# Two-layer graph attention on one core: eight row tiles of the second layer prepared inside the first layer's loop, spread over its odd iterations

## The chip, the cores and the metric

The kernel runs on one core of one Trainium2 chip. The metric is the device time of one execution in microseconds (us), as the median of several runs. The time before the change is 983.33 us (three runs, 982.24 to 983.56). The profiled execution took 982.79 us, and its trace spans 981.0 us.

## The reference

`x` is 4096 x 512 and `adj` is a non-negative 4096 x 4096 matrix, all float32. Two layers follow each other, each with a residual:

```python
# layer 0: attention inside 32 graphs of 128 nodes each
h = relu(layernorm(x))
q, k, v = h @ Wq.T + bq, h @ Wk.T + bk, h @ Wv.T + bv
a = where(mask, q @ k.T * scale, 0)               # mask: both nodes in one graph
scores = (a + adj + adj) * where(mask, 1, -1e6)   # masked softmax over all 4096 columns
x = x + (softmax(scores) * mask) @ v
# layer 1: graph attention with 8 heads of 64
h = relu(layernorm(x))
mx = einsum('nf,hfd->hnd', h, W)                  # per head projection
logits = s_i[:, :, None] + t_j[:, None, :]        # s_i, t_j: mx against two vectors
attn = softmax(where(adj > 0, logits, -inf))
x = x + (attn @ mx, heads side by side)
```

In layer 1 the term `s_i` cancels in the softmax, so a row of the output is a sum over its neighbours j of `exp(t_j) * mx_j`, divided by the sum of `exp(t_j)`. The kernel computes it in this form.

## The kernel before, in words

Rows are handled in 32 tiles of 128. The kernel has four stages.

**Fold.** The query and key weights are multiplied into one matrix (`fold`, L163), so that the scores need one projection and not two.

**Layer 0** is the loop over `g` from 0 to 15 (L523), two row tiles in each iteration. An iteration holds, in program order: the transfer of a later pair of `x` tiles (`load_pair`, L498); the scores of the pair (L464); the projection for the next pair (`queries`, L406, 32 matmuls in the trace); the transpose of the scores and its copy out of PSUM (`turned`, L483 and L485); and for each of the two tiles a pass over a later tile of `adj` (`read`, L425), the product of scores and values with the residual (`attend`, L491 and L493), the store of the new row tile to the DRAM tensor `x1_d` (L496), and the value projection of the next pair (`values`, L418, 8 matmuls for each tile). At its end the pair after the next is normed and transposed (`normed`, L121 and L127).

`read` takes a tile of `adj` in two halves of 1 MB from a ring of seven buffers (`AB = 7`). VectorE turns each half into bytes (L136), ScalarE reads it with an exponential whose sum is the masked part of the denominator (L441, the tile `junk`), and the bytes go to the DRAM tensor `a_d` (L447).

**Preparing layer 1.** For each row tile `normed1(i)` loads the row tile from `x1_d` (L362), norms it (VectorE L114 and L116, GpSimd L118 and L120, VectorE L121), transposes it on TensorE (L127) and takes it out of PSUM on ScalarE (L128). `prepare(i, ...)` projects it (L244, 16 matmuls in the trace, into two PSUM tiles `pp`), takes the exponential of `t_j` (ScalarE L372), multiplies the projection with it (VectorE L253, twice), and splits the result into two float32r parts (ScalarE L231, GpSimd L232), which stay in SBUF as `part0` to `part31`. A tile is always normed one step ahead of its projection. `row1`, `hT1` and `e` have two buffers each (pool `sb2`). The projections share four PSUM buffers (`pp`, pool `ps_p`) with `queries`, `values` and `attend`.

Before the change the only iteration of the loop that does such work is the last one: `prepare_on` (L536) acts if `last`. Its four calls norm tiles 0 to 3 and prepare tiles 0 to 2. The other 29 are prepared in a loop of their own after layer 0 (L567). Parts 0 to 7 lie in the pool `lo`, in memory that the fold has left. Parts 8 to 31 lie in the pool `hi`, which is opened when layer 0's pools are closed (L562) and uses their memory. The weights of the projection, `w1x`, are loaded and extended on VectorE by `load_w1` (L149, products L157 and sums L158), in iteration 2.

**Aggregating layer 1** (L588): for each of 32 row tiles the bytes of `adj` come back from `a_d` (`mw`, L266), VectorE transposes them in blocks (L271) and casts them (L278), and TensorE multiplies them with all parts (L284, 96 matmuls for each tile). A check that the graphs are the row tiles (`graphs_are_tiles`, L300 on) belongs to the second tile of this loop.

The order on each engine is not the order of the source alone. A scheduler orders the instructions when the kernel is built: it takes the earlier line first among those that its model of the engines holds ready. It fixes one order for each engine[...]. So the first block transposes of the aggregation and the check of the graphs stand among the instructions of the preparation.

Of the kernel before, what the change touches and what calls it, by code (L numbers as in the profile page):

```python
# [51 lines left out]
def kernel(  # L52
# [96 lines left out]
    def load_w1(pool, tmp):  # L149

        w = pool.tile([P, KC, WX], F32, name="w1x")
        nc.sync.dma_start(w[:, :, :D], w1.rearrange("(k p) m -> p k m", p=P))
        a_sb = tmp.tile([P, D], F32, name="a_sb", bufs=1)
        nc.sync.dma_start(a_sb, a_dst.to_broadcast([P, D]))
        for k in range(KC):
            wa = tmp.tile([P, D], F32, name="wa", bufs=1)
            nc.vector.tensor_tensor(wa, w[:, k, :D], a_sb, ALU.mult)  # L157
            nc.vector.tensor_reduce(  # L158
                w[:, k, D:], wa.rearrange("p (h d) -> p h d", d=HD), AX.X, ALU.add
            )  # L160
        return w
# [180 lines left out]
    with ExitStack() as straight:  # L342
# [4 lines left out]
        with ExitStack() as prep:  # L347
# [3 lines left out]
            def part_tile(pool, j):  # L351
                if j >= LO:
                    return pool.tile([P, CB, 2, CW1], F32R, name=f"part{j}")
                if j % 2 == 0:
                    two.append(pool.tile([P, 2, CB, 2, CW1], F32R, name=f"part{j}", tag="lo"))
                return two[-1][:, j % 2]
# [3 lines left out]
            def normed1(i):  # L360
                row = sb2.tile([P, D], F32, name="row1")
                nc.sync.dma_start(row, x1_d[i])  # L362
                norm(row, row)
                hT = sb2.tile([P, KC, P], F32, name="hT1")
                relu_T(ps_t, row, hT)
                return hT

            def prepare(i, hT, part):
                pm = project1(ps_p, hT, w1x)
                e = sb2.tile([P, EW], F32, name="e")  # L370
                nc.gpsimd.memset(e[:, EC:], 1.0)
                nc.scalar.activation(e[:, ES:EC], pm[1][:, HW : HW + H], AF.Exp)  # L372
                nc.gpsimd.tensor_copy(e_all[:, i, :], e[:, ES:EC])
                weigh(e, pm)
                split(e, part)
                parts.append(part)

            with (
# [21 lines left out]
                def queries(hT):  # L400

                    gT = sb.tile([P, KC, G * P], F32, name="gT")
                    for m in range(KC):
                        pp = ps_p.tile([P, D], F32, name="pp")
                        for k in range(KC):
                            nc.tensor.matmul(  # L406
                                pp[:, : G * P], m_sb[:, k, ts(m, P)], hT[:, k, :],
                                start=(k == 0), stop=(k == KC - 1),
                            )
                        nc.scalar.activation(  # L410
                            gT[:, m, :], pp[:, : G * P], AF.Identity, bias=c_sb[:, m : m + 1]
                        )
                    return gT
# [11 lines left out]
                def read(i, diag, sums):  # L425


                    a8 = sb.tile([P, N], FP8, name="a8", bufs=3)
                    n = 1
                    for h in range(2):  # L430
                        a, base = aa[2 * i + h], h * NH
                        mask_bytes(a8, a, h)
                        own = i * P - base
                        pieces = ((0, NH),)
                        if 0 <= own < NH:
                            nc.gpsimd.tensor_copy(diag, a[:, ds(own, P)])
                            pieces = ((0, own), (own + P, NH))
                        for c0, c1 in pieces:
                            if c0 < c1:
                                junk = sb.tile([P, NH], BF16, name="junk", bufs=1)  # L440
                                nc.scalar.activation(  # L441
                                    junk[:, c0:c1], a[:, c0:c1], AF.Exp, scale=2.0 * NEG,
                                    accum_out=sums[:, n : n + 1],
                                )
                                n += 1
                        if h:
                            nc.sync.dma_start(a_d[i], a8.bitcast(F32))  # L447
                        if 2 * i + h + AB < 2 * NT:
                            aa[2 * i + h + AB] = load_adj(ap, 2 * i + h + AB)
                    return n  # L450

                def seen():
                    return (
                        sb.tile([P, G, P], F32, name="diag", bufs=3),
                        [small.tile([P, 4], F32, name="sums", bufs=8) for _ in range(G)],
                        [],
                    )

                def scores(g, hT, gT, r, diag, sums, counts):

                    pss = ps_s.tile([P, G, P], F32, name="pss")
                    for t in range(G):
                        for k in range(KC):
                            nc.tensor.matmul(  # L464
                                pss[:, t, :], gT[:, k, ts(t, P)], hT[:, k, ts(t, P)],
                                start=(k == 0), stop=(k == KC - 1),
                            )
                    s = sb.tile([P, G, P], F32, name="s")
                    nc.vector.scalar_tensor_tensor(s, diag, 2.0, pss, ALU.mult, ALU.add)
                    for t in range(G):  # L470
                        nc.scalar.activation(
                            s[:, t, :], s[:, t, :], AF.Exp, bias=r[:, t : t + 1],
                            accum_out=sums[t][:, 0:1],
                        )
                        rsum = rs_all[:, G * g + t : G * g + t + 1]
                        nc.vector.tensor_reduce(rsum, sums[t][:, : counts[t]], AX.X, ALU.add)
                        nc.vector.reciprocal(rsum, rsum)
                    return s

                def turned(s):  # L480
                    ps = ps_s.tile([P, G, P], F32, name="pss")
                    for t in range(G):
                        nc.tensor.transpose(ps[:, t, :], s[:, t, :], ident)  # L483
                    sT = sb.tile([P, G, P], F32, name="sT")
                    nc.scalar.copy(sT, ps)  # L485
                    return sT
# [11 lines left out]
                def load_pair(g):  # L498
                    xg[g] = sb.tile([P, G, D], F32, name="xg", bufs=3)
                    nc.sync.dma_start(  # L500
                        xg[g], x[g * G * P : (g + 1) * G * P, :].rearrange("(t p) d -> p t d", p=P)
                    )
# [20 lines left out]
                for g in range(NG):  # L523
                    last = g + 1 == NG
                    if g + 2 < NG:
                        load_pair(g + 2)
                    if g == 2:
                        w1x = load_w1(pool1, sb)
                    nlook = seen()

                    def look_on(t):
                        if not last:
                            i = G * (g + 1) + t
                            nlook[2].append(read(i, nlook[0][:, t, :], nlook[1][t]))

                    def prepare_on():  # L536
                        if last:
                            i = len(ahead)
                            ahead.append(normed1(i))
                            if i:  # L540
                                prepare(i - 1, ahead[i - 1], part_tile(lo, i - 1))

                    s = scores(g, hT, gT, r, *look)
                    prepare_on()
                    prepare_on()
                    if not last:
                        ngT = queries(nhT)
                    sT = turned(s)
                    nvs = []
                    for t in range(G):  # L550
                        look_on(t)
                        attend(sT, vs[t], g, t)
                        prepare_on()
                        if not last:
                            nvs.append(values(nhT, t))
                    if not last:
                        hT, r, gT, vs, look = nhT, nr, ngT, nvs, nlook
                    if g + 2 < NG:
                        nhT, nr = normed(g + 2)
# [347 lines left out]
```

## Time and profile before

| stage (chain of waits) | from, us | to, us |
|---|---|---|
| start, fold, first norms | 0 | 56.16 |
| layer 0, iterations 0 to 14 | 56.16 | 340.15 |
| iteration 15 and preparation | 340.15 | 480.30 |
| aggregation, end | 480.30 | 981.0 |

| engine | busy us | share of the span |
|---|---|---|
| TensorE matmul | 947.1 | 97% |
| VectorE | 461.6 | 47% |
| ScalarE | 261.6 | 27% |
| GpSimd | 180.3 | 18% |

The profile page gives the busy time of each engine, and cuts the span into 40 slices with the busy share, the granted TensorE clock and the traffic of the DMA engines. The chain of waits is the chain of work that ended last, followed back from the end. The timeline lists the instructions of one engine in order, with the idle time ahead of each and the instruction that ended it. A loop iteration can be found in these views by its scores matmuls (L464), which stand at 56.16, 74.86, 93.56, 113.43 and so on up to 340.15 us.

### The profile page before, as it was taken

Reading aid. Unit: us, or ns where it says so; the run is one execution under the profiler, and the core shown is the slowest. Engines: PE = TensorE matmul, PEld = TensorE weight load, DVE = VectorE, ACT = ScalarE, POOL = GpSimd, SP = SyncE. Lnnn points to the kernel's source line nnn. Section 1 sums busy time; section 2 is a strip of 40 time slices with the busy share of each in tenths; the row PEclk is TensorE's granted clock in tenths of the full one; section 3 lists DMA queues with packets and bytes.
Section 4 is the critical chain, followed back from the end, with each engine's and each line's share of the span. In section 5 each row is a group of like instructions: output and inputs, shape, how many; then the busy total and the mean of one; then the engine's idle time right before and its main releaser. Section 6 shows DMA issues by size and latency. Waiting matters only on the chain.

```text
span 981.0 us, 13168 instructions
## 1 busy us (share of the span) xinstructions
PE 947.1 (97%) x5051; PEld 820.8 (84%) x5051; DVE 461.6 (47%) x982; ACT 261.6 (27%) x501; POOL 180.3 (18%) x344
## 2 busy tenths in 40 slices
PE   6899999999999998999999999999999999999995
PEld 4477666766776676888899999999999999999995
DVE  3756866776675287655232423324233242342421
ACT  3676666676671222333100000000000000000000
POOL 1111211221121055555201101011010110101100
PEclk9899999999999998999999999999999999999998
DMA  9949898998992142222013133131221312312111
GB/s 347 419 181 370 352 370 333 377 367 346 368 371 77 59 129 80 65 65 70 6 43 87 50 81 83 47 86 50 80 85 45 86 51 80 86 44 86 50 38 36
DMA packets 58043, 148.28 MB, mean 151 GB/s; under 512 B 6387, under 2 KB 23027, under 8 KB 49779
## 3 DMA queue, kind: packets, MB, share of 16 engines
q1 hardware_dynamic: 48178, 130.31, 38.2%
q10 hardware_dynamic: 9792, 17.05, 4.6%
q8 instruction: 41, 0.67, 0.3%
q14 instruction: 32, 0.25, 0.1%
HBM read 113.77 MB, written 33.55 MB: 150 GB/s over the span
## 4 chain that ended last, share of the span: by engine, by line
PE 86%; DMA 4%; DVE 4%; ACT 3%; POOL 1%; issue 1%; SPq 0%; ACTq 0%; DVEq 0%
PE pg L284 50%; PE pp L418 10%; PE pp L244 9%; PE pp L406 8%; PE pp L491 3%; DMA a<-adj 3%; PE pss L464 2%; PE pt L127 2%; PE pp L190 2%; ACT junk L441 1%; DMA xg<-x 1%; ACT gT L410 1%; POOL part L232 1%; DVE row L121 1%; POOL rstd L120 0%
## 5 line engine op out<-in xcount | busy, mean ns | idle before, releaser
L284 PE MATMUL pg<-part,at 128*128 128x348 f32 x3072 | 489.0, 321 | 1.2 <-DVE e L253 1.2
L284 PEld LDWEIGHTS pg<-part,at 128*128 128x128 f32 x3072 | 488.7, 188 | 1.6 <-issue 1.6
L278 DVE CAST at<-at 128x4096 fp32r<-128x4096 fp8e4 x32 | 73.6, 2301 | 311.6 <-PE pg L284 311.6
L291 ACT COPY tot<-pg 128x522 f32<-128x522 f32 x32 | 19.1, 598 | 469.9 <-PE pg L284 469.9
L441 ACT ACTIVATE junk<-a 128x2048 bf16<-128x2048 f32 (+15 forms) x92 | 124.6, 1355 | 37.4 <-DMA a<-adj 19.4
L244 PE MATMUL pp<-w1x,hT 128*128 128x256 f32 (+1 forms) x512 | 119.5, 387 | 0.0
L418 PE MATMUL pp<-wv,hT 128*128 128x512 f32 x256 | 116.8, 599 | 1.0 <-ACT hT L128 1.0
L406 PE MATMUL pp<-hT,m_sb 128*128 128x256 f32 x512 | 113.2, 379 | 0.0
L244 PEld LDWEIGHTS pp<-w1x,hT 128*128 128x128 f32 x512 | 96.5, 193 | 14.3 <-issue 0.5
L406 PEld LDWEIGHTS pp<-hT,m_sb 128*128 128x128 f32 x512 | 96.1, 190 | 12.9 <-issue 0.5
L418 PEld LDWEIGHTS pp<-wv,hT 128*128 128x128 f32 x256 | 49.1, 193 | 62.0 <-issue 60.4
L136 DVE TENSOR_SCALAR a<-a 128x512 fp8e4<-128x512 f32 x256 | 94.6, 453 | 7.3 <-DMA a<-adj 4.7
L593 POOL COPY den_all<-tot 128x1 f32<-128x1 f32 x31 | 5.8, 186 | 368.2 <-DVE tot L292 368.2
L128 ACT ACTIVATE hT<-pt 128x512 f32<-128x512 f32 x64 | 37.7, 599 | 82.3 <-PE pt L127 82.3
L602 POOL TENSOR_TENSOR tot<-tot,row 128x512 f32<-128x512 f32 x31 | 40.0, 1289 | 62.0 <-DVE tot L297 62.0
L118 POOL TENSOR_SCALAR ve<-mv 128x1 f32<-128x1 f32 x64 | 16.2, 255 | 178.6 <-DVE mv L116 164.8
L232 POOL TENSOR_TENSOR part<-e,part 128x522 fp32r<-128x522 f32 x32 | 42.0, 1312 | 31.4 <-ACT part L231 27.8
L422 DVE TENSOR_TENSOR v<-pp,bv_sb 128x512 f32<-128x512 f32 x32 | 22.1, 691 | 42.3 <-PE pp L418 42.3
L271 DVE STREAM_TRANSPOSE at<-mw 128x1024 f32<-128x1024 f32 x32 | 39.6, 1238 | 0.0
L253 DVE TENSOR_TENSOR e<-pp,e 128x256 f32<-128x256 f32 x64 | 26.7, 418 | 25.3 <-ACT e L372 22.8
L410 ACT ACTIVATE gT<-pp,c_sb 128x256 f32<-128x256 f32 x64 | 29.9, 469 | 31.5 <-PE pp L406 31.4
L120 POOL TENSOR_TENSOR rstd<-ve,neghalf 128x1 f32<-128x1 f32 x64 | 36.8, 578 | 4.6
(94 smaller groups left out, 594.7 us busy)
## 6 DMA issues: line engine op xcount, KB each, us to landing
a<-adj SPq DMA_DIRECT2D x64, 1024.0 KB, 11.9
a_d<-a SPq DMA_DIRECT2D x32, 512.0 KB, 10.2
row<-x_d SPq DMA_DIRECT2D x64, 256.0 KB, 3.4
mw<-a_d SPq DMA_DIRECT2D x128, 128.0 KB, 4.0
xg<-x SPq DMA_DIRECT2D x16, 512.0 KB, 4.6
x_d<-x ACTq DMA_DIRECT2D x32, 256.0 KB, 4.3
out<-tot ACTq DMA_DIRECT2D x31, 256.0 KB, 3.8
wkT_sb<-wkT SPq DMA_DIRECT2D x4, 256.0 KB, 4.6
```

Source lines behind the costliest of these rows:

```text
L128: nc.scalar.activation(dst, pt, AF.Relu)
L136: nc.vector.tensor_scalar(a8v[:, u], av[:, u], 0.0, None, ALU.is_gt, saturate=False)
L232: nc.gpsimd.tensor_sub(dst[:, :, 1, :], e3, dst[:, :, 0, :].bitcast(F32))
L244: nc.tensor.matmul(pm[g][:, :n], hT[:, k, :], w1x[:, k, g * HW : g * HW + n], start=(k == 0), stop=(k == KC - 1),)
L271: nc.vector.transpose(at8.rearrange("p c n b -> p (c n b)").bitcast(F32).rearrange("p (c u n) -> p c u n", c=NW, n=B), mw.rearrange("p u ( ...
L278: nc.vector.tensor_copy(at.rearrange("p (c b) q -> p c b q", b=BY), at8.rearrange("p c q b -> p c b q"))
L284: nc.tensor.matmul(pg[:, c, : 2 * CW1], at[:, j, :], part(j)[:, c].rearrange("p s w -> p (s w)"), start=(j == 0), stop=(j == NT - 1),)
L406: nc.tensor.matmul(pp[:, : G * P], m_sb[:, k, ts(m, P)], hT[:, k, :], start=(k == 0), stop=(k == KC - 1),)
L410: nc.scalar.activation(gT[:, m, :], pp[:, : G * P], AF.Identity, bias=c_sb[:, m : m + 1])
L418: nc.tensor.matmul(pp, hT[:, k, ts(t, P)], wv[:, k, :], start=(k == 0), stop=(k == KC - 1))
L441: nc.scalar.activation(junk[:, c0:c1], a[:, c0:c1], AF.Exp, scale=2.0 * NEG, accum_out=sums[:, n : n + 1],)
L602: nc.gpsimd.tensor_add(num, num, row)
```

## The change

`prepare_on` takes a condition. It is called in three places: after the scores in the last iteration; after `turned` in the odd iterations from 3 to 15; and after the first `attend` in the last iteration. So iterations 3, 5, 7, 9, 11 and 13 each norm one row tile of layer 1 and prepare the one before it (iteration 3 only norms tile 0), which prepares tiles 0 to 4. The last iteration prepares tiles 5, 6 and 7 and norms up to tile 8. The loop after layer 0 begins at tile 8 and has 24 tiles, where it had 29. The weights `w1x` are loaded in iteration 1. The purpose is to give TensorE work of layer 1 during layer 0, from row tiles that are long finished, and to leave less of it for the stage between the layers.

```diff
@@ -524,7 +524,7 @@
-                    if g == 2:
+                    if g == 1:
                         w1x = load_w1(pool1, sb)
@@ -533,24 +533,24 @@
-                    def prepare_on():
-                        if last:
+                    def prepare_on(now):
+                        if now:
                             i = len(ahead)
                             ahead.append(normed1(i))
                             if i:
                                 prepare(i - 1, ahead[i - 1], part_tile(lo, i - 1))
 
                     s = scores(g, hT, gT, r, *look)
-                    prepare_on()
-                    prepare_on()
+                    prepare_on(last)
                     if not last:
                         ngT = queries(nhT)
                     sT = turned(s)
+                    prepare_on(3 <= g and g % 2)
                     nvs = []
                     for t in range(G):
                         look_on(t)
                         attend(sT, vs[t], g, t)
-                        prepare_on()
+                        prepare_on(last and t == 0)
                         if not last:
                             nvs.append(values(nhT, t))
```

## The prediction

> **What bounds the kernel now.** I read the page first, for which engine is full and where.
>
> ```profile
> PE 947.1 (97%) x5051; PEld 820.8 (84%) x5051; DVE 461.6 (47%) x982; ACT 261.6 (27%) x501; POOL 180.3 (18%) x344
> PE   6899999999999998999999999999999999999995
> PEclk9899999999999998999999999999999999999998
> ```
>
> TensorE is busy 97% of the span. Its only slice after the start that falls short is the sixteenth (about 368 to 392 us), and the clock row dips there too. That is the passage from layer 0 to the preparation. A change that adds no TensorE work and removes none can gain only what TensorE loses: it stands idle or runs at a lower clock. So the question is how much it loses in each stage that the change touches. The timeline of TensorE shows an idle gap only where it has one. Layer 0 has four of note:
>
> ```profile
> 104.19 0.66 PE L127 MATMUL pt<-ident,hn 128*128 128x128 f32 x4 [1.28 <-DVE hn L121]
> 160.90 1.12 PE L491 MATMUL pp<-v,sT 128*128 128x512 f32 x2 [0.27 <-ACT sT L485]
> 199.55 1.12 PE L491 MATMUL pp<-v,sT 128*128 128x512 f32 x2 [1.32 <-ACT sT L485]
> 238.09 1.12 PE L491 MATMUL pp<-v,sT 128*128 128x512 f32 x2 [1.19 <-ACT sT L485]
> ```
>
> The first is iteration 2, where the extension of `w1x` takes VectorE ahead of a norm. The other three lie in iterations 5, 7 and 9, each at the first `attend`, which waits for the copy of the turned scores. The timeline of ScalarE tells why that copy is late at 199:
>
> ```profile
> 196.65 0.63 ACT L441 ACTIVATE junk<-a 128x512 bf16<-128x512 f32 x1 [0.72 <-DMA a<-adj]
> 197.41 1.38 ACT L441 ACTIVATE junk<-a 128x1408 bf16<-128x1408 f32 x1
> 199.14 0.36 ACT L485 COPY sT<-pss 128x256 f32<-128x256 f32 x1
> ```
>
> ScalarE's fixed order puts a read of `adj` ahead of the copy, and the read waits for its transfer. As a check, the scores of iteration 0 stand at 56.16 us and those of iteration 15 at 340.15 us. That is 283.99 us for 15 iterations. An undisturbed one takes 132.13 - 113.43 = 18.70 us, so 15 take 280.5, and layer 0 loses 3.5 us in all. The gaps of iterations 5, 7 and 9 are 0.27 + 1.32 + 1.19 = 2.8 us of it.
>
> The passage between the stages loses more (timeline of TensorE, then stretches of 4 us with clock):
>
> ```profile
> 357.57 0.66 PE L127 MATMUL pt<-ident,row 128*128 128x128 f32 x4 [1.24 <-DVE row L121]
> 371.39 1.12 PE L127 MATMUL pt<-ident,row 128*128 128x128 f32 x4 [3.27 <-DVE row L121]
> 389.46 0.66 PE L127 MATMUL pt<-ident,row 128*128 128x128 f32 x4 [0.49 <-DVE row L121]
> ```
>
> ```profile
> 368.00:372.00 4.00, 0.73 (x4) 0.61 (x4) 3.58 (x9) 0.71 (x2) 2.70 (x8) 0.82 0.11 20
> 372.00:376.00 4.00, 4.00 (x14) 3.33 (x13) 3.04 (x9) 1.49 (x3) 0.73 (x2) 0.50 0.21 68
> 376.00:380.00 4.00, 4.00 (x16) 3.34 (x16) 2.69 (x5) 0.40 (x2) 1.52 (x3) 0.83 0.51 147
> ```
>
> In a row the columns are TensorE, weight loads, VectorE, ScalarE, GpSimd, then the clock. After a gap of 3.27 us the clock is 0.50 for 4 us and 0.83 for 4 more, which costs 2.0 + 0.7 = 2.7 us beyond the gap. From 340.15 to 393.0 us (52.9 us) TensorE projects ten tiles. In the even stretch after it a tile takes 3.95 us (the chain has its projections at 401.07, 405.01, 408.96). Ten tiles and the scores, transposes and products of iteration 15 (1.79 + 0.2 + 1.9) come to 43.4 us. So the passage loses about 9.5 us. Of that 5.2 are idle gaps on `row L121` and about 3 are clock. From 393 to 479 us nothing is lost.
>
> [...] 0.50 after a gap of 3.27 us, and 1.00 around the gaps of 1.2 to 1.3 us in layer 0. [...] the split L232 (median 1.23 us) took 3.22 us at 352.88, under the cast L278. [...]
>
> **The change, part by part.**
>
> Moved: five tiles of preparation (29 after the loop become 24). On TensorE that is 5 x 3.95 = 19.7 us taken from after layer 0 and added inside it. The sum on TensorE is zero. The last iteration prepares three tiles before and after.
>
> Gaps of iterations 5, 7 and 9: the call is placed behind `turned` and ahead of the first `attend`, in odd iterations. So 3.5 us of projections (16 matmuls) come to stand between the turned scores and the `attend` that waits for their copy. The copy may then be 3.5 us later without a gap, and the three gaps are at most 1.32 us. Also, every odd iteration grows by 3.95 us while the bytes of `adj` stay the same, so the reads wait less. I count -2.8 us; the bounds are -2.8 and 0.
>
> Other engines in layer 0: one tile costs VectorE 0.69 + 0.18 + 0.55 + 2 x 0.42 = 2.3 us (L114, L116, L121, L253), up to 3.2 where L121 takes 1.44 as it does at 369.90; ScalarE 0.60 + 0.18 + 0.63 = 1.4 us; GpSimd 0.22 + 0.57 + 1.23 + 0.3 = 2.3 us. VectorE is busy 14.3 of 20 us there, or 13.4 of an iteration of 18.7; an odd iteration has 13.4 + 3.2 = 16.6 of 22.65. ScalarE has 12.7 + 1.4 = 14.1. Neither becomes the bound, and the cost is hidden under TensorE.
>
> Added waits. The transposes of a row tile of layer 1 wait for L121. Its row was stored two or more iterations earlier and its transfer takes 3.4 us, so it can be ready long before. The two `pp` buffers of a projection come free only after L372 and both L253, which stand behind reads of `adj` in the lists of ScalarE and VectorE. Behind them TensorE has the first `attend` and the first `values` on the other two buffers, 0.86 + 3.43 = 4.3 us, and then the second `attend` wants one of the two. A read that waits longer than that would stop TensorE. The waits of `junk` on `a<-adj` total 14.7 us in 21 waits, the longest 1.8 us. So mostly nothing, sometimes one gap like those of now. The bounds are 0 and five gaps of 1.3 us = 6.5 us; I take +0.8.
>
> `w1x` one iteration earlier: the same 4 products and 4 sums of 0.68 us, against the same kind of norm. I take 0, with the present gap of 1.28 us as bound to either side.
>
> The passage: what disturbs it stays. The block transposes (three of 1.23 us), casts (two of 2.3 to 2.5 us) and the check of the graphs (16 operations of 0.42 us) are 15 us of VectorE work, which stands in its list among the norms. Their first input waits for memory of layer 0 to come free, so they come when layer 0 ends, now or after the change. A norm must be ready every 3.95 us, and a row must be loaded (3.4 us), normed (about 3) and transposed within two tiles, 7.9 us. That leaves about 1 us for foreign work. So again several us are lost. The order will be a new one, and the long gap with its half clock (6 us together) may be shorter or double. In favour of shorter: in the last iteration there is one row fewer to norm. I take -0.7, with bounds of -6 and +6.
>
> Tiles 8 on now come straight after layer 0, into memory that layer 0 has just left. The last store of `x1` takes 4.3 us to land, while the first split into that memory comes about 8 us after the last `attend` (projections of tiles 7 and 8). I take 0, and up to 3 us if it is held.
>
> Sum: -2.8 + 0.8 + 0 - 0.7 + 0 = -2.7, so 983.3 - 2.7 = 980.6 us.
>
> **The rivals.**
>
> A, the forecast above (gaps of layer 0 go, the passage stays about as it is): about 980.6, chance 0.40.
>
> B, the passage gets through without a gap long enough to lower the clock. It then loses about 3.5 where it lost 9.5, and layer 0 gains 2: 983.3 - 6 - 2 = 975.3. For it: one gap makes up most of the loss. Against it: the same VectorE work comes at the same place. Chance 0.20.
>
> C, new gaps in layer 0 on `pp` or on the copies cost what the old ones did, and nothing else moves: 983. For it: VectorE and ScalarE run close behind their transfers. Against: their slack above. Chance 0.15.
>
> D, slower: the new order in the passage has a second long gap, or the first splits wait for layer 0's memory: +6 and -2 give 987. For it: a pair of tiles has only about 1 us of slack, and the loop after layer 0 loses its five tiles in memory that is free from the start. Against: nothing is added there. Chance 0.25.
>
> **How the numbers follow.** Faster by over 0.2% means below 981.4. All of B, most of A (0.34) and little of C give 0.56. Slower by over 0.2% is above 985.3: D, with some of it inside the bound, and a little of C, 0.25. The rest is 0.19. The range takes in B and D: 974 to 987.5.
>
> **What would show it.** Right: no gap on the copy `sT` (L485) in iterations 5, 7 and 9; the scores of successive iterations 18.70 and 22.65 us apart in turn from iteration 4 on; gaps on `row L121` of some 5 us in the passage with the clock at 0.5 once. Wrong: gaps in odd iterations ahead of the second `attend` or at `queries`; ScalarE's L231 waiting for a store at tile 8; a passage with no half clock, or with two.

## The result and the profile after

| | before, us | after, us | ratio, 95% interval |
|---|---|---|---|
| measured with the prediction (4 runs each) | 983.44 | 980.59 | 0.9967, 0.9944 to 0.9989 |
| measured again (41 and 13 runs) | 983.12 | 980.2 | 0.997, 0.9956 to 0.9985 |

The change makes the kernel about 3 us faster, 0.3%. The profiled execution after the change spans 976.9 us, 4.1 us less than the one before.

Three rows of the page of the changed kernel:

```profile
PE 944.0 (97%) x5051; PEld 818.9 (84%) x5051; DVE 460.5 (47%) x982; ACT 260.1 (27%) x501; POOL 185.2 (19%) x344
PE   6899999999999998899999999999999999999995
PEclk9799999999999999999999999999999999999998
```

TensorE runs the same 5051 matmuls. Its busy row still falls below nine tenths in the slices of the passage, now the sixteenth and seventeenth. The clock row no longer dips there. The timeline of TensorE after the change shows these gaps from the first scores to the last projection (the number in brackets is the idle time ahead of the instruction, then what ended it):

```profile
86.78 1.12 PE L491 MATMUL pp<-v,sT 128*128 128x512 f32 x2 [1.24 <-ACT sT L485]
143.82 1.12 PE L491 MATMUL pp<-v,sT 128*128 128x512 f32 x2 [0.56 <-ACT sT L485]
227.30 1.12 PE L491 MATMUL pp<-v,sT 128*128 128x512 f32 x2 [0.80 <-ACT sT L485]
373.82 0.65 PE L127 MATMUL pt<-ident,row 128*128 128x128 f32 x4 [0.38 <-DVE row L121]
387.42 0.66 PE L127 MATMUL pt<-ident,row 128*128 128x128 f32 x4 [3.02 <-DVE row L121]
396.30 0.66 PE L127 MATMUL pt<-ident,row 128*128 128x128 f32 x4 [1.20 <-DVE row L121]
404.17 0.66 PE L127 MATMUL pt<-ident,row 128*128 128x128 f32 x4 [1.53 <-DVE row L121]
```

The gaps of iterations 5, 7 and 9 are gone. The first three rows are iterations 1, 4 and 8, all without projections. The gaps of layer 0 come to 2.6 us, where they were 4.1 us. In the passage the gaps remain: 6.1 us in sum, where they were 5.2 us. So the passage did not gain from shorter gaps.

Where the time went, by the starts of the scores of iterations 0 and 15 and the start of the aggregation:

| | before, us | after, us | difference |
|---|---|---|---|
| start to scores of iteration 0 | 56.0 | 56.9 | +0.9 |
| iterations 0 to 14 | 284.0 | 301.4 | +17.4 |
| iteration 15 and preparation | 140.3 | 117.9 | -22.4 |
| aggregation, end | 500.7 | 500.7 | 0.0 |

The work that moved is five projections of 3.51 us and the transposes of six row tiles of 0.44 us, 20.2 us in all. (The transposes of one row tile and a quarter stood ahead of iteration 15 before the change, and those of seven and a quarter do now.) Layer 0 grew by 17.4 us for it, so layer 0 runs 2.8 us better. The passage shrank by 22.4 us, so it runs 2.2 us better in this pair of profiles; the experiments show that this second part is the clock of the two executions. The start is not touched by the change; it lay between 53.7 and 57.7 us in the profiles of this study.

The gain in layer 0 of 2.8 us is more than the 1.5 us by which its gaps fell. The chain of waits of the changed kernel shows iteration 6, without projections, and iteration 7, with them:

```profile
183.71 0.47 ACT gT L410
184.19 0.27 ACT sT L485
184.46 0.04 issue
184.50 1.12 PE pp L491 x2
...
203.03 3.51 PE pp L244 x16
206.54 0.87 PE pp L491 x2
```

In iteration 6 the chain leaves TensorE for the copies on ScalarE, and the first `attend` takes 1.12 us; the iteration lasts 18.70 us. In iteration 7 the projections run up to the `attend`, which takes 0.87 us. Iteration 7 lasts 22.31 us, although 18.70 + 3.95 would be 22.65. From these numbers an undisturbed iteration holds a wait of about 0.34 us that its timeline doesn't list as a gap, and the projections cover that too. The experiment `odd_scores` below tests this.

### The profile page after: what moved, and what is told of

Read it like the earlier page. It is cut to its first block, busy times and chain, and to the rows that moved or that the text cites. A ratio compares the mean times of both kernels' runs of the same rounds, so it can differ in the third digit from the quotient of the medians.

```text
span 976.9 us, 13164 instructions
## 1 busy us (share of the span) xinstructions
PE 944.0 (97%) x5051; PEld 818.9 (84%) x5051; DVE 460.5 (47%) x982; ACT 260.1 (27%) x501; POOL 185.2 (19%) x344
## 4 chain that ended last, share of the span: by engine, by line
PE 87%; DMA 4%; DVE 3%; ACT 2%; POOL 2%; issue 1%; SPq 0%; ACTq 0%; DVEq 0%; POOLq 0%
PE pg L284 50%; PE pp L418 10%; PE pp L406 9%; PE pp L244 8%; DMA a<-adj 3%; PE pp L491 3%; PE pss L464 2%; PE pt L127 2%; PE pp L190 2%; ACT junk L441 1%; POOL part L232 1%; DMA xg<-x 1%; DVE row L121 0%; DVE a L136 0%; ACT gT L410 0%
## 5 line engine op out<-in xcount | busy, mean ns | idle before, releaser
L244 PE MATMUL pp<-w1x,hT 128*128 128x256 f32 (+1 forms) x512 | 117.3, 383 | 0.0
L128 ACT ACTIVATE hT<-pt 128x512 f32<-128x512 f32 x64 | 37.0, 598 | 76.6 <-PE pt L127 76.4
```

The lines of the kernel that those rows point to most:

```text
L128: nc.scalar.activation(dst, pt, AF.Relu)
L244: nc.tensor.matmul(pm[g][:, :n], hT[:, k, :], w1x[:, k, g * HW : g * HW + n], start=(k == 0), stop=(k == KC - 1),)
```

## The experiments

Layer 0 and the passage of each profiled execution are set side by side first. To compare them, the moved work is taken out of layer 0 and added to the passage (20.2 us where eight tiles are prepared before the loop behind layer 0, 19.6 us for `even`, which has transposed fewer row tiles by then, 12.3 us for `half`). Beside each stands what TensorE lost there: the sum of its listed gaps, and the time that the half clock cost (half of its length: 1.7 us where the clock was 0.50 for 3.4 us).

| kernel | time, us | layer 0 less moved work | gaps, clock | passage plus moved work | gaps, clock |
|---|---|---|---|---|---|
| before | 983.12 | 284.0 | 4.1, 0 | 140.3 | 5.2, 3.4 |
| `w1_only` | 986.07 | 286.7 | 5.3, 1.7 | 139.2 | 5.2, 1.7 |
| changed | 980.59 | 281.2 | 2.6, 0 | 138.1 | 6.1, 0 |
| `after_again` | 980.2 | 281.3 | 2.8, 0 | 139.2 | 5.6, 1.7 |
| `w1_late` | 979.56 | 280.7 | 2.5, 0 | 139.2 | 5.5, 1.7 |
| `half` | 980.88 | 282.8 | 3.9, 0 | 139.1 | 5.5, 1.7 |
| `odd_scores` | 982.05 | 282.9 | 2.9, 0 | 138.9 | 5.6, 1.7 |
| `even` | 981.65 | 286.4 | 6.6, 1.7 | 139.1 | 5.6, 1.7 |
| `before_graphs` | 978.96 | 284.5 | 4.9, 0 | 134.9 | 3.0, 0 |
| `after_graphs` | 975.71 | 280.7 | 2.2, 0 | 133.8 | 2.3, 0 |
| `graphs_w2` | 975.63 | 280.5 | 2.3, 0 | 133.7 | 2.3, 0 |
| `after_graphs_row3` | 978.3 | 286.2 | 6.3, 1.7 | 131.8 | 0.8, 0 |
| `graphs_row3_w2` | 978.38 | 286.2 | 4.6, 3.4 | 131.8 | 0.8, 0 |
| `graphs_row3_w3` | 976.73 | 282.1 | 3.7, 0 | 131.8 | 0.8, 0 |

The experiments ran on three chips. The kernel before took 983.12, 982.65 and 983.43 us on them, and each ratio below is against the kernel before on the same chip.

The table is nearly a sum. Take 279.9 us (layer 0 of the kernel before without its gaps), add the gaps and the lost clock, and take off 0.34 us for each iteration that has projections behind `turned`: this meets layer 0 of all fourteen profiles within 0.4 us. The passage without its gaps and lost clock is 131.0 to 132.3 us in all of them.

**The changed kernel once more: is the passage better, or only its clock?** No edit.

> The changed kernel itself, profiled and timed once more. If the gain is a saving in layer 0 (theory 1: the projections fill TensorE's wait between the turned scores and the first attend in odd iterations), the stretch from the scores of iteration 0 to those of iteration 15 is again about 301.4 us, and the time is 980 to 981. If the gain hangs on the clock not falling in the passage (theory 2), this profile may show a half clock after a gap of some 3 us there, the passage is then some 3 us longer, and the time of some executions is near 983.

Measured: 980.2 us, ratio 0.997 (0.9956 to 0.9985). Layer 0 took 301.5 us. The passage took 1.1 us longer than in the first profile. Stretches of 4 us, where the third number from the end is the clock; first the changed kernel, then its second profile:

```profile
384.00:388.00 4.00, 0.98 (x7) 0.59 (x6) 3.07 (x7) 0.70 (x2) 3.67 (x10) 1.00 0.01 1
388.00:392.00 4.00, 4.00 (x22) 3.42 (x21) 3.46 (x9) 2.00 (x4) 1.04 (x2) 1.00 0.51 131
```

```profile
384.00:388.00 4.00, 1.32 (x6) 0.78 (x5) 3.07 (x6) 0.70 (x2) 3.86 (x7) 1.00 0.18 43
388.00:392.00 4.00, 3.66 (x15) 3.15 (x16) 3.46 (x11) 0.60 (x1) 1.25 (x5) 0.66 0.20 66
```

The same gap of 3.02 us is followed by a clock of 1.00 once and by 0.66 the other time, with 22 and 15 matmuls in the next stretch. Theory 1 holds for layer 0. Of theory 2 remains that the difference between the two executions' passages is the clock, 1.7 us, less 0.6 us of shorter gaps: they have the same list of instructions.

**The earlier load of `w1x` alone.**

```diff
-                    if g == 2:
+                    if g == 1:
                         w1x = load_w1(pool1, sb)
```

> The kernel before with w1x loaded in iteration 1, and nothing else. Theories 1 and 2: the gap of 1.28 us moves from iteration 2 to 1, the gaps of iterations 5, 7 and 9 stay, and the time is 983.4 within 1 us. Theory 3 (the earlier load is what helps): 981 or less.

Measured: 986.07 us, ratio 1.003 (1.0017 to 1.0043). This misses all theories: it is slower by some 3 us. Layer 0 of the profile is 2.7 us longer: its gaps grew by 1.2 us, and behind the gap of 2.09 us the clock was at half for 3.4 us, which cost 1.7. The timeline of TensorE shows these gaps, and one more of 0.48 us in iteration 6:

```profile
87.17 1.12 PE L491 MATMUL pp<-v,sT 128*128 128x512 f32 x2 [1.08 <-ACT sT L485]
200.41 1.13 PE L491 MATMUL pp<-v,sT 128*128 128x512 f32 x2 [1.02 <-ACT sT L485]
221.47 1.12 PE L491 MATMUL pp<-v,sT 128*128 128x512 f32 x2 [2.09 <-ACT sT L485]
298.06 1.13 PE L491 MATMUL pp<-v,sT 128*128 128x512 f32 x2 [0.58 <-ACT sT L485]
```

The gap at 221 is in iteration 8, long after the load. The copy `sT` needs these transposes of TensorE, which end at 218.5 us:

```profile
218.12 0.38 PE L483 MATMUL pss<-ident,s 128*128 128x128 f32 x2
```

The timeline of ScalarE there, first of this kernel and then of the kernel before in the same iteration:

```profile
218.79 1.91 ACT L441 ACTIVATE junk<-a 128x2048 bf16<-128x2048 f32 x1 [1.20 <-DMA a<-adj]
...
221.06 0.36 ACT L485 COPY sT<-pss 128x256 f32<-128x256 f32 x1
```

```profile
217.51 0.36 ACT L485 COPY sT<-pss 128x256 f32<-128x256 f32 x1
...
218.28 1.90 ACT L441 ACTIVATE junk<-a 128x2048 bf16<-128x2048 f32 x1
```

Before, the copy comes ahead of a read of `adj`; here a read that waits for its transfer comes ahead of the copy, which starts some 2.6 us after its input is there. So an edit in iteration 1 gives ScalarE another order seven iterations later, and TensorE waits for it. Its passage has the same gaps as before (1.24, 3.27, 0.19 and 0.48 us).

**The same tiles, the call in another place.**

```diff
-                    prepare_on(last)
+                    prepare_on(last or (3 <= g and g % 2))
...
-                    prepare_on(3 <= g and g % 2)
+                    prepare_on(last)
```

> The changed kernel with the same tiles in the same odd iterations, but the call placed after the scores and ahead of the queries. Theory 1: the first attend has its wait for the copy of the turned scores back, so an odd iteration is 18.70 + 3.95 = 22.65 us and not 22.31, and gaps ahead of the first attend of odd iterations can come back; layer 0 is 2 to 4 us longer than in the changed kernel, 303.4 to 305 us, and the time about 983. Theory 2 (the place does not matter, only the passage does): layer 0 stays at 301.4 and the time follows the passage.

Measured: 982.05 us, ratio 0.9995 (0.9982 to 1.0008). Layer 0 took 303.05 us, a little under the range of theory 1. Iterations 5, 7, 11 and 13 took 22.64, 22.53, 22.99 and 22.64 us, where the changed kernel has 22.31 or 22.32 in each of them. The chain of waits of this kernel in iteration 7:

```profile
206.81 0.22 PE pss L483 x2
207.03 0.66 PE pt L127 x6
207.69 1.08 PE pp L491 x2
```

The `attend` has its longer duration back, 1.08 us. Of the gain of 2.9 us only about 1 is left, and the interval includes none. In the profile it is 1.1 us, just what the listed gaps fell by (4.1 to 2.9 us); there is no gap in iterations 5, 7 and 9 here either. The place behind `turned` carries the rest, the five waits of 0.34 us, as theory 1 has it.

**Even iterations.**

```diff
-                    prepare_on(3 <= g and g % 2)
+                    prepare_on(last or (4 <= g and g % 2 == 0))
```

> The changed kernel with the calls after turned in iterations 4, 6, 8, 10, 12 and 14 and not in the odd ones. The same tiles are moved. Theory 1: an even iteration becomes 22.31 us as the odd one was, so layer 0 again saves about 0.36 us for each of five tiles; the gaps on the copy now fall where no projections stand, up to 1.3 us each: layer 0 is 301 to 304 us. If the odd iterations were needed (the reads of adj late in just those), it is at the upper end. The passage has another order; its loss is open between 4 and 10 us, and so is the time, 979 to 986.

Measured: 981.65 us, ratio 0.9992 (0.9977 to 1.0006). Layer 0 of the profiled execution took 306.1 us, beyond the range expected. But that execution took 984.37 us, 2.7 us above the median, and 1.7 us of its layer 0 are a half clock of 3.4 us behind the first gap below. Iterations 6 and 10 took 22.32 us, so the small saving is there. The gaps of layer 0 by the timeline of TensorE:

```profile
87.68 2.07 PE L491 MATMUL pp<-v,sT 128*128 128x512 f32 x2 [2.58 <-ACT sT L485]
146.40 1.12 PE L491 MATMUL pp<-v,sT 128*128 128x512 f32 x2 [0.62 <-ACT sT L485]
207.80 0.44 PE L127 MATMUL pt<-ident,row 128*128 128x128 f32 x2 [1.75 <-DVE row L121]
291.60 1.12 PE L491 MATMUL pp<-v,sT 128*128 128x512 f32 x2 [1.65 <-ACT sT L485]
```

The second is in iteration 4, which only norms a tile, and the last in iteration 11; no projections stand in either. The third, in iteration 7, is a wait of the added work itself, for the norm of a row of layer 1. By the medians the odd places are the better ones, by about 1.5 us; the single times of `even` lie between 979.2 and 987.8 us, so the size is not well known. Why iteration 1 lost 2.58 us here and 1.24 in the changed kernel was not separated.

**The spread alone.**

```diff
-                    if g == 1:
+                    if g == 2:
                         w1x = load_w1(pool1, sb)
```

> The changed kernel with w1x loaded in iteration 2 as before, so with the spread preparation alone. If the earlier load costs in the changed kernel what it cost alone (layer 0 2.7 us longer), layer 0 is some 299 us and the time 977.5. If the longer odd iterations take that cost up, layer 0 stays at 301.5 and the time at 980.2. If tile 0 now waits for w1x in iteration 5, layer 0 is longer by 1 us or more.

Measured: 979.56 us, ratio 0.9961 (0.9947 to 0.9975). Layer 0 took 300.9 us, 0.5 us less than in the changed kernel. So the earlier load, which cost 3 us by itself, costs about half a microsecond beside the spread in these profiles; the intervals of the times overlap and don't show it. It is the spread preparation that gains, 3.1 us alone. Layer 0 gained 3.3 us by the table, and its two parts make up the whole: the gaps fell from 4.1 to 2.5 us, and five waits of 0.34 us are 1.7 us.

**Half of it.**

```diff
-                    prepare_on(3 <= g and g % 2)
+                    prepare_on(7 <= g and g % 2)
```

> The changed kernel with calls in iterations 7, 9, 11 and 13 only, so three tiles prepared in layer 0 and six before the loop behind it, where the changed kernel has five and eight. Theory 1 (a saving of 0.34 us for each odd iteration with projections, and the gaps on the copy in them): relative to the changed kernel two savings of 0.34 are lost and the gaps of iterations 5 and 7, up to 1.5 us together, can come back; iterations 9, 11 and 13 are 22.31 us and iteration 5 is 18.70 or more. The time is 981 to 982.5. If the saving lies in the passage alone, the time is again 980.2.

Measured: 980.88 us, ratio 0.9978 (0.9965 to 0.9991), just under the range expected. Iterations 9, 11 and 13 took some 22.32 us each; iterations 6, 7 and 10, without projections, had gaps of 0.76, 0.84 and 0.97 us. The passage has the same four gaps (0.38, 3.02, 0.62 and 1.53 us) as with eight tiles. How many tiles are moved does not change what the passage loses.

**What the passage loses: the check of the graphs moved into layer 0.** The check is the same, in 16 pairs of half the size, and `held` is set at the start.

```diff
+                    if g == 13:
+                        graphs_are_tiles(sb)
...
             if i == 1:
-                graphs_are_tiles(sb3)
```

> The changed kernel with the check of the graphs done in iteration 13 of layer 0 (in 16 pairs of half the size, which a full SBUF asks for) and not in the passage. If the gaps on row L121 come from foreign VectorE work among the norms, 6.6 us less of it leave gaps of 2 to 4 us where there are 5.6 to 6.1, and no half clock if the gap of 3.0 us is one of those that shrink: passage 114.5 to 117 us where it is 118 to 119, time 977 to 978.5. [...]

Measured: 975.71 us, ratio 0.9932 (0.9918 to 0.9945), better than expected. The passage took 113.6 us, some 5 us less. In this run's timeline of TensorE (its lines stand one further down: L128 is L127):

```profile
371.59 0.66 PE L128 MATMUL pt<-ident,row 128*128 128x128 f32 x4 [0.38 <-DVE row L122]
383.84 0.66 PE L128 MATMUL pt<-ident,row 128*128 128x128 f32 x4 [1.91 <-DVE row L122]
```

Two gaps of 2.3 us in sum are left of four with 5.6 to 6.1, and the clock stays at 1.00. VectorE work of 6.6 us among the norms cost 3.3 to 3.8 us of gaps and the clock behind them. Part of this gain is lost again: the aggregation takes 502.1 to 503.0 us in the six kernels with the moved check, and 500.6 to 501.1 us in the others. Why was not separated.

**The same in the kernel before.** The same edit on the kernel before.

> The kernel before with the check of the graphs done in iteration 13 and not in the passage; nothing is spread. If the passage's gaps have the same cause in both kernels (the check among the norms), the passage shrinks as it did in the changed kernel, by about 5 us to 134 to 136, layer 0 stays at 284, and the time is 977.5 to 979: then the spread preparation and this are independent, and each adds its own gain. If the spread preparation was what made room for the check, this gains 2 us or less.

Measured: 978.96 us, ratio 0.9963 (0.9949 to 0.9976). The passage took 134.9 us, 5.4 us less, and layer 0 284.5 us. The gaps of the passage fell from 5.2 to 3.0 us, and the clock stayed at 1.00. Moving the check and spreading the preparation add up: on the same chip the spread kernel with the moved check (`graphs_w2`, below) took 975.63 us, which is again about 3 us for the spread.

**A third row buffer.** `bufs=3` for `row1`, on top of the moved check. To make room, `w1x` is extended in halves of 256 columns.

```diff
-                row = sb2.tile([P, D], F32, name="row1")
+                row = sb2.tile([P, D], F32, name="row1", bufs=3)
```

> The same with three buffers for row1 and not two (and w1x extended in halves of 256 columns, to make room). If the gaps come from the round of a row (load 3.4 us, norm about 3, transpose) in two tiles, a third buffer gives about 4 us more slack, and the gaps of the passage nearly go: passage 112.5 to 114.5 us, time 974.5 to 977. If VectorE is simply full at these moments, or the norm's order is fixed too late, it changes nothing against the run with the check moved alone.

Measured: 978.3 us, ratio 0.9951 (0.9935 to 0.9968), slower than expected. The passage shrank to 111.6 us, even a little more than expected; one gap is left in it:

```profile
388.00 0.66 PE L128 MATMUL pt<-ident,row 128*128 128x128 f32 x4 [0.78 <-DVE row L122]
```

But layer 0 took 306.4 us, with gaps of 2.33 and 1.76 us in iterations 1 and 2 and a half clock of 3.4 us behind the first. The next three runs move the load of `w1x` (`g == 2` or `g == 3` in the place of `g == 1`), first without and then with the third buffer.

> The changed kernel with the check moved and w1x loaded in iteration 2. If the parts add up: 975.7 less the 0.6 us that the later load gave, so 974.5 to 976.

Measured: 975.63 us, ratio 0.9933 (0.9913 to 0.9953), as expected, and not to be told from `after_graphs`. These two are the fastest here.

> The same with the third row buffer and w1x extended in halves. In the run with w1x in iteration 1 the passage was 111.6 us but layer 0 had two gaps of 2.3 and 1.8 us and a half clock at the extension. If the later place avoids these, layer 0 is 301 us and the time 972 to 974.5. If extending in halves costs them wherever it stands, layer 0 is 304 to 306 and the time about 978.

Measured: 978.38 us, ratio 0.9951 (0.9936 to 0.9967). Layer 0 again took 306.4 us: four gaps of 3.3 us in sum and a half clock of 6.8 us now lie in iterations 2 and 3.

> The same with w1x in iteration 3, which is still two iterations ahead of its first use. As the run before, 972 to 974.5 if the place decides; if tile 0's projection in iteration 5 waits for the extension, there is a gap at L244's first matmuls there.

Measured: 976.73 us, ratio 0.9942 (0.9922 to 0.9962). Layer 0 took 302.25 us, with a gap of 2.20 us in iteration 4. That is between the two times expected. So the third buffer helps the passage by 2 us, and layer 0 loses 1.5 to 5.6 us, most of it in its first iterations. Whether the halves or the other layout in memory do that was not separated.

## Why the prediction was right, and where its steps were not

The time was predicted at 980.6 us and measured at 980.59 and 980.2 us. The main step was right: projections put ahead of an `attend` that waits for its copy save TensorE time in layer 0. That the sum met the median so closely is luck. Layer 0 gained 2.8 us where the terms for it gave 2.0, and the 0.7 us forecast for the passage is not there when executions with the same clock are compared.

- **Gaps of iterations 5, 7 and 9, -2.8 us: right that they go.** In ten profiles no iteration with projections behind `turned` has a gap on the copy, 48 iterations in all. Whether the place removed these three is not shown: `odd_scores` has none in iterations 5, 7 and 9 either (one of 0.41 us stands in iteration 11). The prediction's second reason, that a longer iteration leaves the reads of `adj` more time, may have been enough.
- **New gaps, +0.8 us: too small, and the place wrong.** The prediction looked for them ahead of the second `attend`, on the `pp` buffers. None came there. They came on the copy in iterations 4 and 8, 0.56 + 0.80 = 1.36 us. How many gaps the iterations without projections have differs with every edit; no run explains their number.
- **A term was missing.** "18.70 and 22.65 us apart in turn" was wrong: with projections it is 22.31. The wait of 0.34 us in every undisturbed iteration was counted as work. Over five iterations it is worth 1.7 us, more than half of what layer 0 gained.
- **`w1x` earlier, 0 with 1.28 us to either side: wrong as a bound.** Alone it costs about 3 us. The step took only the extension's own gap and not the new order of the reads. In the changed kernel the term is about 0.5 us by the profiles.
- **The passage, -0.7 us: not shown, and its reason wrong.** "One row fewer to norm" did not shorten the gaps; their sum rose from 5.2 to 5.6 or 6.1 us. `w1_only` has the passage of the kernel before and lost 1.7 us of clock in it, as `after_again` did: both take 139.2 us. The six profiles `w1_only`, `after_again`, `w1_late`, `half`, `odd_scores` and `even` move all, some or none of the work and have passages of 138.9 to 139.2 us. The first profiles of before and after differ by 2.2 us because the half clock cost 3.4 us in one and nothing in the other (the prediction counted 2.7 for the first), which is more than the added 0.9 us of gaps. The cause named, foreign VectorE work among the norms, is shown for the check of the graphs by `after_graphs` and `before_graphs`. For the block transposes and casts it was not tested.
- **Tile 8 in memory of layer 0, 0: right.** ScalarE's L231 waits only for VectorE there, at most 3.1 us, and for no store.
- **Rivals.** B's way (a passage without half clock, 975.3) is what the moved check gives, 975.7 with the clock at 1.00, and not what the change gives. D (slower) did not come. Nor did C: the gaps of layer 0 did not come back in full.

## What to carry to other kernels

Work moved to a full engine gains nothing by being moved; it gains by standing where that engine waits for another engine's short answer, and such a wait can hide in a period that looks undisturbed (about 0.34 us in 18.70 here, an estimate from the times of iterations 6 and 7). Add up the work of one period and compare it with the period before calling it full. Where a scheduler fixes each engine's order, an edit far away can put a waiting instruction ahead of one that the bound engine needs (in `w1_only` the copy started 2.6 us after its input was there), so time each part of a change alone.

## What the runs showed of the hardware

The clock of TensorE fell after shorter gaps than the one of 3.27 us in the kernel before. In `even` it fell behind a single gap of 1.97 us. Stretches of 2 us of that kernel:

```profile
406.00:408.00 2.00, 0.40 (x2) 0.00 (x1) 1.41 (x4) 0.00 (x0) 1.91 (x5) 1.00 0.00 0
408.00:410.00 2.00, 1.63 (x6) 1.52 (x7) 1.66 (x5) 0.51 (x2) 0.22 (x1) 0.61 0.00 0
```

Six matmuls run in the second stretch; 11 did from 400 to 402 us at a clock of 1.00. A gap of 2.09 us in `w1_only` was followed by 0.50, while behind gaps of 2.20 us in `graphs_row3_w3` and of 3.02 us in the first profile of the changed kernel the clock stayed at 1.00. So the length of a gap alone does not decide.

For the two profiles of the changed kernel the difference is where the gap lies. In the profile of the kernel before the clock changed at 15.57, 18.98, 36.05, 42.88, 370.56, 377.38 and 971.30 us; the times from each to the next are 1, 5, 2, 96, 2 and 174 times 3.413 us. In the first profile of the changed kernel it changed at 14.11, 17.52, 34.59, 44.83 and 969.84 us, which is 1, 5, 3 and 271 times 3.413 us. Counted in steps of 3.413 us from such a change, an execution falls into stretches, and the idle time of TensorE can be added up in each:

| execution | stretch from, us | TensorE idle in it, us | clock in the next stretch |
|---|---|---|---|
| changed, first profile | 382.75 | 1.77 | 1.00 |
| changed, first profile | 386.16 | 1.25 | 1.00 |
| `even` | 405.04 | 1.97 | 0.50 |
| `w1_only` | 219.38 | 2.09 | 0.50 |
| `after_again` | 385.90 | 2.44 | 0.50 |
| before | 367.15 | 2.44 | 0.50 |

The gap of 3.02 us of the changed kernel fell across the edge of two stretches in the first profile, and mostly into one in the second. For the gap of 2.20 us in `graphs_row3_w3` this was not shown. Between the first scores and the aggregation the fourteen profiles have eleven falls of the clock. For ten of them the idle time in the 3.41 us ahead can be worked out from the gaps and the clock of stretches of 4 us, and it is 1.97 to some 2.7 us; for the fall in `odd_scores` it lies between 1.8 and 2.5 us. The half clock then lasted 3.4 us, or 6.8 us in the kernel before and in `graphs_row3_w2`, where TensorE was idle for another 0.83 us in the first half of it. Ahead of the first scores the clock also fell behind less: behind 1.34 us at 36.05 us in the kernel before, and behind 1.22 us at 34.59 us in the changed one. So idle time is not all that counts.

So two executions of one kernel can differ by a microsecond or more: the two of the changed kernel differ by 1.7 us of clock in the passage, with the same gap of 3.02 us in both.
